# An involution and two Winograd convolutions on one core: involution by halves, low parts on VectorE, batch-norm sums on ScalarE

## The chip, the core and the metric

The kernel runs on 1 core of one Trainium2 chip. The time is that of one execution on the device, in microseconds. The core's engines are TensorE (PE, with PEld for its weight loads), VectorE (DVE), ScalarE (ACT), GpSimd (POOL) and SyncE (SP, which here only issues DMAs). Each engine runs its own list of instructions in order and waits on semaphores for the others.

## What is computed

Input x has 8 images of 256 channels, 56 x 56, in float32. Two residual blocks follow each other, each on a group norm of its input.

```python
def gn(v):                                  # 32 groups of 8 channels
    g = v.reshape(B, 32, C // 32, H, W)
    return ((g - mean(g)) / sqrt(var(g) + 1e-5)).reshape(v.shape)

def involution(x):                          # K = 7, G = 16 groups of 16 channels
    ker = einsum('bchw,oc->bohw', x, w_reduce) + b_reduce        # 64 channels
    ker = einsum('bchw,oc->bohw', ker, w_span) + b_span          # 16 * 49 channels
    ker = ker.reshape(B, 16, 1, 49, H, W)
    patches = all 49 shifts of pad(x, 3), reshaped to (B, 16, 16, 49, H, W)
    return (ker * patches).sum(axis=3).reshape(B, C, H, W)

def tri_conv(x, w):                         # 3 x 3, padding 1
    tq = ternary_quantize(w - mean(w))      # -1, 0 or 1, thresholds from max and min
    return conv(x, tq) + einsum('bchw,oc->bohw', x, tq[:, :, 1, 1])

def conv_block(x):
    out1 = relu(batch_norm(tri_conv(x, w1), g1, b1))             # over the whole batch
    return relu(out1 + batch_norm(tri_conv(out1, w2), g2, b2))

x = x + involution(gn(x))
x = x + conv_block(gn(x))
```

## The kernel before

The program goes through five stages. Everything is unrolled. Data dependencies become semaphores, and a scheduler puts each engine's instructions in order, near to the order of the text.

**Start.** `prep` of image 0, and `quantize` (L154) twice: it loads a weight tensor, finds the thresholds with DVE and POOL, makes the ternary weights, transforms them (six matrices a weight tensor, Winograd style) and stores them to DRAM (`wqd`). The working tile of `quantize` lies in the memory that the involution's `apool` and `qpool` take over afterwards.

**Involution (L578 to L609)**, by chunks: image b, channel tile t of 128 channels. The image is cut into patches of 3 x 8 pixels, 19 rows (`ty`) of 7 patches. A patch together with its border is 9 x 14 = 126 input pixels (`NQ`), which lie on the partitions. For each chunk:
- `generate` (L517) makes `a`, a [126, 133 patches, 8 groups x 24 pixels] tile: for every group and pixel of a patch the matrix that maps the 126 input pixels to the output pixel. It takes 32 steps. A step writes the products for three pixels and two groups (six float32 matmuls, L534, weights of 64 x 126, 133 columns each, two row halves of the array side by side; each float32 matmul is two load-and-multiply records in the trace) into one accumulator tile `pg`. DVE adds the bias on the way to `a` (L546), in every fourth step ACT does (L542).
- `apply_rows` (L552) then goes through ten pairs of patch rows. For each row it takes a tile `q` of 126 pixels x 7 patches x 128 channels, and 28 small matmuls (L560, weights 126 x 32, 48 columns). ACT (L568), DVE (L570) and POOL (L575) put the result onto x in SBUF.
- `load_q` (L508) loads a `q` tile, 441 KB in pieces of 512 bytes, from `xed`, a copy of the normed image in DRAM in which neighbouring patches' borders are repeated. It is issued on SP; six tiles are in hand (`NQB`).
- `prep` (L451), for the next image, runs in ten strips of six rows, one after each apply step of the chunk t = 1: POOL norms the strip (L457), PE reduces it to `kr` (L463, ACT L476), transposes it (L481, ACT L486), ACT's queue stores it to `xtd` (L489), and `expand` (L441), on SP, copies it into `xed`, DRAM to DRAM, two strips later.
- `params` (L405) computes the next image's group norm in two apply steps of the chunk t = 0; `group_norm_params` (L120) at the chunk's end computes that of the result (seven `bn_stats` on DVE, L124, two tiny matmuls, L128 and L135, and some DVE operations), and the result goes to DRAM (`x1d`, L609).

All accumulators of the stage come from one pool of four tiles (L388).

**Convolutions 1 and 2 (`conv_phase`, L214).** 16 half images each. `transform` (L243) norms the half image into `xp` with ACT (L619 or L629), builds six combinations of rows `r` with DVE (L261, L281 to L295), and `keep` (L263) splits each into a rounded high part `hi` (ACT, L266) and the rest `lo` (POOL, L267). The transform of half n + 1 is spread over the matmuls of half n. For each of the six, 24 matmuls (L343, 128 x 128, 392 columns) fill one of four accumulators; ACT copies two of them out (`e`, L350), DVE combines them to the output `y` (L353 to L369), takes its statistics (L375, eight `bn_stats`), and SP stores it (L377). The batch norm follows from the statistics (`batch_norm_params`, L142), once all halves are done.

**Final pass (L637 to L649).** It reads y1, y2 and x1, and writes the output.

## Time and profile before

| | us |
|---|---|
| median of 3 runs (2721.05 to 2726.63) | 2722.48 |
| the profiled execution | 2720.13 |
| its span, first to last instruction | 2718.0 |
| PE busy | 1841.0 |
| DVE busy | 1835.3 |
| ACT busy | 913.3 |
| POOL busy | 734.2 |

The profile's page gives for each engine its busy time, and a list of the costliest groups of instructions: source line, engine, operation, output tile and inputs, shapes, number, then busy time and the mean duration of one in ns, and after the bar the time that the engine stood idle just before them, with what ended it. A tile's name stands without its buffer number, so `pa` are all accumulators of apply. "issue" as a releaser means that the engine waited for nothing that the profile shows. In a timeline a row has its start and its length in us, the engine, line, tiles and the number of instructions merged into it, and in brackets the idle time before it. PEclk is the granted clock of TensorE as a share of full speed; the DMA share is the mean busy share of the core's 16 DMA engines.

### The profile page before, as it was taken

The numbers are of one execution on the slowest core, as the hardware profiler recorded it, in microseconds if no ns is written. First come the engines' busy times: TensorE is split into PE (matmuls) and PEld (weight loads), VectorE is DVE, ScalarE is ACT, GpSimd is POOL, SyncE is SP. The second block draws the span as 40 slices with busy tenths as digits, with TensorE's granted clock in tenths as the row PEclk, the third lists the DMA queues.
The fourth block names the chain that finished last, engine by engine and source line by source line (L and its number), as shares of the span: only waits on it lengthen the run. The fifth ranks groups of instructions, "written<-read, shape, count | busy, mean of one in ns | idle before, by whom it ended". The sixth has DMA issues, their size and how long they took to land.

```text
span 2718.0 us, 65147 instructions
## 1 busy us (share of the span) xinstructions
PE 1841.0 (68%) x28676; PEld 1727.9 (64%) x28676; DVE 1835.3 (68%) x2499; ACT 913.3 (34%) x1819; POOL 734.2 (27%) x701
## 2 busy tenths in 40 slices
PE   3147667687776768777648899998499898992000
PEld 2137566676665667666548889898498898992000
DVE  4575354564644455553449999999599999995444
ACT  2023324243342434333223433333143333422333
POOL 2001212121121212112115444454154454440000
PEclk9567879788786878778779999999799999996555
DMA  6436786767678576757763233221423222217998
GB/s 238 177 123 168 227 229 191 225 193 232 174 236 241 173 230 190 232 151 226 198 189 115 97 117 123 98 97 72 166 93 119 103 97 97 98 79 313 428 429 382
DMA packets 343531, 500.64 MB, mean 184 GB/s; under 512 B 11496, under 2 KB 308678, under 8 KB 327314
## 3 DMA queue, kind: packets, MB, share of 16 engines
q1 hardware_dynamic: 306320, 424.76, 47.4%
q10 hardware_dynamic: 36930, 71.74, 7.0%
q8 instruction: 225, 3.69, 0.6%
q14 instruction: 56, 0.46, 0.1%
HBM read 353.49 MB, written 187.92 MB: 199 GB/s over the span
## 4 chain that ended last, share of the span: by engine, by line
PE 31%; DVE 31%; DMA 17%; issue 15%; ACT 3%; POOL 1%; SPq 1%; ACTq 0%; DVEq 0%; POOLq 0%
PE pg L534 14%; PE pa L560 9%; DMA q<-xed 5%; DVE y L329 4%; DVE st L375 4%; DVE a L261 3%; PE c L343 3%; PE pk L463 3%; DMA y1f<-y1d 3%; DVE r L295 3%; DVE r L261 2%; DMA out_y<-x1f 2%; DMA x1f<-x1d 2%; PE pt L481 1%; DVE y L360 1%
## 5 line engine op out<-in xcount | busy, mean ns | idle before, releaser
L343 PE MATMUL c<-pl,wq 128*128 128x392 f32 x4608 | 909.7, 362 | 142.6 <-ACT e L350 79.3
L343 PEld LDWEIGHTS c<-pl,wq 128*128 128x128 f32 x4608 | 896.1, 199 | 155.9 <-ACT e L350 89.1
L267 POOL TENSOR_TENSOR pl<-r,pl 128x812 fp32r<-128x812 f32 x192 | 469.2, 2468 | 525.5 <-ACT pl L266 448.9
L560 PE MATMUL pa<-a,q 126*32 126x48 f32 x17024 | 316.1, 244 | 275.2 <-issue 200.4
L560 PEld LDWEIGHTS pa<-a,q 126*32 126x32 f32 x17024 | 280.2, 138 | 311.8 <-issue 251.6
L534 PE MATMUL pg<-kr,wl 64*126 64x133 f32 x6144 | 403.6, 293 | 40.3 <-DVE a L546 35.5
L534 PEld LDWEIGHTS pg<-kr,wl 64*126 64x126 f32 x6144 | 394.6, 200 | 46.4 <-DVE a L546 35.8
L570 DVE SCALAR_TENSOR_TENSOR inv<-pa,half_sb,inv 128x168 f32<-128x168 f32 x304 | 105.7, 388 | 446.5 <-ACT inv L568 446.3
L546 DVE TENSOR_TENSOR a<-pg,bt 126x798 f32<-126x798 f32 x384 | 370.5, 1044 | 25.9 <-PE pg L534 13.1
L575 POOL TENSOR_TENSOR x<-x,inv 128x168 f32<-128x168 f32 (+1 forms) x304 | 156.2, 533 | 765.5 <-DVE inv L570 761.2
L266 ACT CAST pl<-r 128x812 fp32r<-128x812 f32 x192 | 166.7, 871 | 494.6 <-DVE r L281 342.1
L542 ACT ACTIVATE a<-pg,bt 126x133 f32<-126x133 f32 x768 | 230.3, 482 | 288.5 <-PE pg L534 187.2
L568 ACT ACTIVATE inv<-pa,half_sb 128x336 f32<-128x336 f32 (+1 forms) x160 | 84.2, 526 | 474.6 <-PE pa L560 469.9
L457 POOL TENSOR_SCALAR xn<-x,gn 128x336 f32<-128x336 f32 (+1 forms) x160 | 95.9, 608 | 314.9 <-PE pt L481 251.1
L261 DVE SCALAR_TENSOR_TENSOR a<-xp 128x812 f32<-128x812 f32 x64 | 173.2, 2738 | 0.0
L463 PE MATMUL pk<-xn,wr 128*128 128x336 f32 (+1 forms) x320 | 131.2, 540 | 25.9 <-POOL xn L457 23.2
L375 DVE BATCH_NORM_STATS2 st<-y 128x6 f32<-128x392 f32 x256 | 122.6, 549 | 0.0
L124 DVE BATCH_NORM_STATS2 st_b<-x 128x6 f32<-128x448 f32 x112 | 69.7, 623 | 73.5 <-POOL x L575 73.4
L629 ACT ACTIVATE xp<-raw,bi_bn,sc_bn 128x392 f32<-128x392 f32 (+1 forms) x128 | 84.7, 720 | 65.8 <-DVE a L261 51.1
L619 ACT ACTIVATE xp<-raw,gn 128x392 f32<-128x392 f32 (+1 forms) x128 | 84.5, 720 | 53.8 <-DVE a L261 45.2
L476 ACT ACTIVATE kr<-pk,br 128x112 f32<-128x112 f32 (+1 forms) x232 | 74.6, 455 | 80.1 <-PE pk L463 79.3
L646 DVE SCALAR_TENSOR_TENSOR y1f<-y2f,sc_bn,y1f 128x3136 f32<-128x3136 f32 x16 | 55.7, 3484 | 65.5 <-DMA y2f<-y2d 65.5
(115 smaller groups left out, 1508.5 us busy)
## 6 DMA issues: line engine op xcount, KB each, us to landing
q<-xed SPq DMA_DIRECT2D x304, 441.0 KB
xed<-xtd SPq DMA_DIRECT2D x72, 588.0 KB
xtd<-stg ACTq DMA_DIRECT2D x72, 384.0 KB
raw<-x1d SPq DMA_DIRECT2D x32, 812.0 KB
raw<-y1d SPq DMA_DIRECT2D x32, 812.0 KB
x<-in_x SPq DMA_DIRECT2D x16, 1568.0 KB
x1d<-x SPq DMA_DIRECT2D x16, 1568.0 KB
y1d<-y SPq DMA_DIRECT2D x32, 784.0 KB
```

The lines of the kernel that those rows point to most:

```text
L261: nc.vector.scalar_tensor_tensor(dst, x, c, y, ALU.mult, ALU.add)
L266: nc.scalar.copy(hi, r)
L267: nc.gpsimd.tensor_tensor(lo, r, hi.bitcast(F32), ALU.subtract)
L329: nc.vector.scalar_tensor_tensor(yr[k][:, to], x[:, to], c, z[:, to], ALU.mult, op)
L343: nc.tensor.matmul(ps[:, to, :NM], wq[:, k, t, dx, to * P:(to + 1) * P], part[:, t, :, dx:dx + W], start=(c == 0), stop=(c == last))
L375: nc.vector.bn_stats(stats[:, to, n * NST + j, :], y[:, to, j * NM:(j + 1) * NM])
L463: nc.tensor.matmul(pk[:, :n * W], wr[:, t, :], strip[:, t, :n, PAD:PAD + W], start=(t == 0), stop=(t == CT - 1))
L534: nc.tensor.matmul(dst, wl[rows, t, gp, o:o + NQ], kr[rows, py, px].rearrange("r a t -> r (a t)"), start=True, stop=True)
L542: nc.scalar.activation(av[:, g0 + h, p0 + j], ps[:NQ, h, j * NT:(j + 1) * NT], AF.Identity, bias=bt[:, t, g0 + h, p0 + j:p0 + j + 1])
L546: nc.vector.tensor_tensor(av[:, g0:g0 + 2, p0:p0 + 3].rearrange("q g p t -> q g t p"), ps[:NQ, :, :3 * NT].rearrange("q h (t p) -> q h t p ...
L560: nc.tensor.matmul(ps[g * 32:(g + 1) * 32, r, k * 2 * NP:(k + 1) * 2 * NP], q[:NQ, k, g * 32:(g + 1) * 32], a[:NQ, (ty + r) * TX + k, g * ...
L575: nc.gpsimd.tensor_tensor(xv, xv, inv[:, r].rearrange("p t (y x) -> p y t x", y=PY)[:, :m], ALU.add)
```

## The change

Involution: `a` is made for one half of a chunk at a time (10 or 9 patch rows, 70 or 63 patches; two tiles, `a0` and `a1`, of together the same size). `generate` becomes a generator of 16 steps: six pixels and two groups a step, in 12 matmuls of 70 or 63 columns; DVE takes five of the six pixels (one instruction), ACT the sixth (two). The main loop runs over halves. After each apply step of a half it advances `generate` of the next half by three or four steps, then a side task: `params` of the next image, now for both channel tiles at once and cut into five pieces (chunk t = 0, second half), or the strips of `prep` (chunk t = 1: one a step in the first half, two, two, one in the second). `kr` is split into two tiles by halves. `expand` copies a half image in one DMA, so there are two per image, issued in the last half after apply steps 1 and 4. The result's `bn_stats` follow the apply steps; its aggregate and the store to `x1d` come after the first apply step of the next half; the group norm of the result is computed once, for all images, at the end. Five `q` tiles are in hand instead of six, and the first loads of the next image are put on SP at the end of the chunk before. The first half's `generate` stands between the two `quantize`.

Convolutions: `lo` is subtracted on DVE. The eight `bn_stats` of a half image are replaced by four ACT passes over `y` (sum and sum of squares of y less a shift, the shift being the mean of one block of the first half image), one after each of the first four groups of matmuls of the next half (ahead of the copy `e`, where there is one). `batch_norm_params` works from the sums.

The core of the diff (context lines shortened):

```diff
-NT = TY * TX
+HTY = (10, 9)
...
-NQB = 6
+STEPS = 5
+UP, UV = 6, 5
+NU = GP * NP // UP
+NQB = 5
...
+    def image_stats(st, xt, j):
+        nc.vector.bn_stats(st[:, j, :], xt[:, j * NC:(j + 1) * NC])
...
+    def batch_norm_params(stats, shift, gamma, beta, name):
         mv = small.tile([P, CT, 2], F32, tag="bn_mv", name=f"bmv_{name}")
-        for t in range(CT):
-            nc.vector.bn_aggr(mv[:, t, :], stats[:, t, :, :].rearrange("p n s -> p (n s)"))
+        nc.vector.tensor_reduce(mv, stats, AX.X, ALU.add)
+        nc.vector.tensor_scalar(mv, mv, 1.0 / (B * HW), None, ALU.mult)
+        d = small.tile([P, CT], F32, tag="bn_d", name=f"bd_{name}")
+        nc.vector.tensor_tensor(d, mv[:, :, 0], mv[:, :, 0], ALU.mult)
+        nc.vector.tensor_tensor(mv[:, :, 1], mv[:, :, 1], d, ALU.subtract)
+        nc.vector.tensor_tensor(mv[:, :, 0], mv[:, :, 0], shift, ALU.subtract)
...
                 nc.scalar.copy(hi, r)
-                nc.gpsimd.tensor_tensor(lo, r, hi.bitcast(F32), ALU.subtract)
+                nc.vector.tensor_tensor(lo, r, hi.bitcast(F32), ALU.subtract)
...
+        def statistics(n, y):
+            if n == 0:
+                mv = small.tile([P, CT, 2], F32, tag="sh_mv", name=f"sh_mv{i}")
+                for to in range(CT):
+                    st = small.tile([P, 6], F32, tag=f"sh_st{to}", name=f"sh_st{i}_{to}")
+                    nc.vector.bn_stats(st, y[:, to, :NM])
+                    nc.vector.bn_aggr(mv[:, to, :], st)
+                nc.vector.tensor_scalar(shift, mv[:, :, 0], -1.0, None, ALU.mult)
+            for to in range(CT):
+                for j, f in enumerate((AF.Identity, AF.Square)):
+                    dummy = wk.tile([P, NH], F32, tag="dummy", name=f"dummy{i}_{n}_{to}_{j}")
+                    nc.scalar.activation(dummy, y[:, to], f, bias=shift[:, to:to + 1],
+                                         accum_out=stats[:, to, j, n:n + 1])
+                    yield
+        done = iter(())
...
+                next(done, None)
                 if k in (2, 4):
                     e = half("e")
                     nc.scalar.copy(e, m[k])
...
-                for j in range(NST):
-                    nc.vector.bn_stats(stats[:, to, n * NST + j, :],
-                                       y[:, to, j * NM:(j + 1) * NM])
                 nc.sync.dma_start(dst_d[b][to][:, h * NH:(h + 1) * NH], y[:, to])
+            done = statistics(n, y)
+        for _ in done:
+            pass
...
+        def expand(b, h):
             src, dst = xt_d[b % 2][:], xe_d[b % 2][:]
-            n = min(SR, H - s * SR)
+            r0 = h * HTY[0] * PY
+            n = min(HTY[h] * PY, H - r0)
             nc.sync.dma_start(
-                bass.AP(dst.tensor, dst.offset + (PAD + s * SR) * QX * C,
-                        [[EX * C, TX], [QX * C, n], [1, QX * C]]),
-                bass.AP(src.tensor, src.offset + s * SR * WQ * C,
-                        [[PX * C, TX], [WQ * C, n], [1, QX * C]]))
-        def prep(b, pr):
+                bass.AP(dst.tensor, dst.offset + (PAD + r0) * QX * C,
+                        [[QX * C, n], [EX * C, TX], [1, QX * C]]),
+                bass.AP(src.tensor, src.offset + r0 * WQ * C,
+                        [[WQ * C, n], [PX * C, TX], [1, QX * C]]))
...
-                if s > 1:
-                    expand(b, s - 2)
                 yield
-            expand(b, NS - 2)
-            expand(b, NS - 1)
-        prm = [params(0, t, xs[0, t]) for t in range(CT)]
-        for _ in prep(0, prm):
-            pass
-        with tc.tile_pool(name="qp", bufs=1) as qp:
-            quantize(wq_d[0], w1, qp, ps_flat, "w1")
-            quantize(wq_d[1], w2, qp, ps_flat, "w2")
...
+        def generate(b, t, h, a):
+            n = HTY[h] * TX
             av = a[:NQ].rearrange("q t (g p) -> q g p t", g=GT)
+            for u in range(NU):
+                gp, p0 = u // (NP // UP), u % (NP // UP) * UP
+                ps = ps_tile(f"pg_{b}_{t}_{h}_{u}")
+                for j in range(UP):
                     py, px = (p0 + j) // PX, (p0 + j) % PX
                     o = LEAD - py * QX - px
+                    for i in range(2):
+                        rows = slice(i * CR, (i + 1) * CR)
+                        dst = ps[:NQ, i, j:UV * n:UV] if j < UV else ps[:NQ, i, j * n:(j + 1) * n]
                         nc.tensor.matmul(
                             dst, wl[rows, t, gp, o:o + NQ],
+                            kr[h][rows, py, px].rearrange("r a t -> r (a t)"),
                             start=True, stop=True)
                 g0 = 2 * gp
+                nc.vector.tensor_tensor(
+                    av[:, g0:g0 + 2, p0:p0 + UV].rearrange("q g p t -> q g t p"),
+                    ps[:NQ, :, :UV * n].rearrange("q i (t p) -> q i t p", p=UV),
+                    bt[:, t, g0:g0 + 2, p0:p0 + UV].unsqueeze(2).to_broadcast([NQ, 2, n, UV]),
+                    ALU.add)
+                for j in range(UV, UP):
+                    for i in range(2):
+                        nc.scalar.activation(
+                            av[:, g0 + i, p0 + j], ps[:NQ, i, j * n:(j + 1) * n],
+                            AF.Identity, bias=bt[:, t, g0 + i, p0 + j:p0 + j + 1])
+                yield
...
+        queue = [(b, t, ty) for b in range(B) for t in range(CT) for ty in range(TY)]
         loads = {}
         def prefetch(b):
-            while queue and queue[0][0] == b and len(loads) < NQB:
+            while queue and queue[0][0] <= b and len(loads) < NQB:
...
+        for _ in params(0):
+            pass
+        for _ in prep(0):
+            pass
+        for h in range(2):
+            expand(0, h)
+        apool = ph1.enter_context(tc.tile_pool(name="apool", bufs=1))
+        a_next = apool.tile([P, HTY[0] * TX, GT * NP], F32, tag="a0", name="a_0_0_0")
+        with tc.tile_pool(name="qp", bufs=1) as qp:
+            quantize(wq_d[0], w1, qp, ps_flat, "w1")
+            for _ in generate(0, 0, 0, a_next):
+                pass
+            quantize(wq_d[1], w2, qp, ps_flat, "w2")
+        apool1 = ph1.enter_context(tc.tile_pool(name="apool1", bufs=1))
+        qpool = ph1.enter_context(tc.tile_pool(name="qpool", bufs=NQB))
+        halves = [(b, t, h) for b in range(B) for t in range(CT) for h in range(2)]
+        pending = None
+        prefetch(0)
+        for m, (b, t, h) in enumerate(halves):
+            a = a_next
+            gen = iter(())
+            if m + 1 < len(halves):
+                b1_, t1_, h1_ = halves[m + 1]
+                a_next = (apool, apool1)[h1_].tile([P, HTY[h1_] * TX, GT * NP], F32,
+                                                   tag=f"a{h1_}", name=f"a_{b1_}_{t1_}_{h1_}")
+                gen = generate(b1_, t1_, h1_, a_next)
+            if h == 0:
+                st = small.tile([P, NCB, 6], F32, tag="gn_st2", name=f"st2_{b}_{t}")
+                gst[b, t] = (st, 0)
             more = b + 1 < B
+            side, plan = iter(()), (0,) * STEPS
+            if more and t == 0 and h == 1:
+                side, plan = params(b + 1), (1, 1, 1, 1, 1)
+            elif more and t == 1 and h == 0:
+                strips = prep(b + 1)
+                side, plan = strips, (1, 1, 1, 1, 1)
+            elif more and t == 1:
+                side, plan = strips, (2, 2, 1, 1, 0)
+            for i in range(STEPS):
+                apply_rows(b, t, h, a, i)
                 prefetch(b)
+                statistics(b, t, h * HTY[0] + i * QG)
+                if i == 0 and pending is not None:
+                    pending()
+                    pending = None
+                if more and t == 0 and h == 0 and i == 0:
+                    for k in range(CT):
+                        xs[b + 1, k] = load_x(b + 1, k)
+                advance(gen, 4 if i == 0 else 3)
+                advance(side, plan[i])
+                if more and t == 1 and h == 1 and i in (1, STEPS - 1):
+                    expand(b + 1, int(i > 1))
+            for _ in gen:
                 pass
+            for _ in side if (t, h) != (1, 0) else ():
+                pass
+            if h == 1:
+                pending = finish(b, t)
+                prefetch(b + 1 if t == 1 else b)
+        pending()
+        for _ in group_norm_params(mv2.rearrange("p b t s -> p (b t) s"),
+                                   gn2.rearrange("p b t s -> p (b t) s"), ps_flat, "gn2"):
```

## The prediction

> **What bounds the kernel now.** I read the page first, then the sums by stretch of time, cut where the chain of waits changes its kind (first weight quantization to 172 us, involution to 1409, convolution 1 to 1952, convolution 2 to 2467, final pass).
>
> ```profile
> 0.00:172.00 172.00, 32.54 (x156) 24.85 (x156) 94.86 (x118) 18.66 (x43) 15.06 (x31) 0.67 0.51 191
> 172.00:1409.00 1237.00, 897.69 (x23908) 805.95 (x23908) 645.45 (x1258) 427.43 (x1230) 238.52 (x444) 0.80 0.70 201
> 1409.00:1952.00 543.00, 457.29 (x2308) 450.48 (x2308) 492.84 (x553) 186.69 (x258) 244.30 (x116) 0.91 0.30 117
> 1952.00:2467.00 515.00, 453.50 (x2304) 446.66 (x2304) 484.45 (x524) 185.91 (x256) 236.36 (x111) 0.93 0.27 100
> 2467.00:2718.00 251.00, 0.00 (x0) 0.00 (x0) 117.68 (x48) 94.60 (x33) 0.00 (x0) 0.50 0.98 414
> ```
>
> Columns: stretch, its length, busy PE, PEld, DVE, ACT, POOL, granted clock, DMA share. The convolutions are DVE's: 977 of 1058 us busy, with PE at 911. In the involution no engine is full: PE 898 of 1237, DMA 0.70. The final pass is DMA at 0.98, and the change leaves it alone. So the groups by shape for the convolutions, and the timeline of PE for the involution.
>
> ```profile
> L267 POOL TENSOR_TENSOR pl<-r,pl 128x812 fp32r<-128x812 f32 x192 | 469.2, 2468 | 525.5 <-ACT pl L266 448.9 <-DMA raw<-y1d 56.3 <-PE c L343 20.3
> L261 DVE SCALAR_TENSOR_TENSOR a<-xp 128x812 f32<-128x812 f32 x64 | 173.2, 2738 | 0.0
> L375 DVE BATCH_NORM_STATS2 st<-y 128x6 f32<-128x392 f32 x256 | 122.6, 549 | 0.0
> L295 DVE SCALAR_TENSOR_TENSOR r<-u,v 128x812 f32<-128x812 f32 x32 | 77.3, 2415 | 0.0
> L261 DVE SCALAR_TENSOR_TENSOR q<-xp 128x812 f32<-128x812 f32 x32 | 32.5, 1017 | 2.6 <-ACT xp L619 1.7 <-ACT xp L629 0.9
> ```
>
> One DVE form on one shape takes 1.02 us (q) where POOL is idle and 2.74 us (a) where POOL's L267 runs: the difference is waiting for POOL, not work.
>
> ```profile
> 591.56 1.29 PE L560 MATMUL pa<-a,q 126*32 126x48 f32 x98 [1.36 <-issue]
> 598.34 1.22 PE L560 MATMUL pa<-a,q 126*32 126x48 f32 x94 [3.11 <-issue]
> 604.87 1.16 PE L560 MATMUL pa<-a,q 126*32 126x48 f32 x89 [1.30 <-issue]
> 609.21 1.13 PE L560 MATMUL pa<-a,q 126*32 126x48 f32 x85 [0.72 <-issue]
> ```
> ```profile
> 536.49 2.79 PE L560 MATMUL pa<-a,q 126*32 126x48 f32 x127 [3.42 <-issue]
> ...
> 547.02 2.79 PE L560 MATMUL pa<-a,q 126*32 126x48 f32 x128 [1.09 <-issue]
> ```
> ```profile
> 1377.90 2.86 PE L560 MATMUL pa<-a,q 126*32 126x48 f32 x128 [2.51 <-issue]
> ...
> 1405.99 1.04 PE L560 MATMUL pa<-a,q 126*32 126x48 f32 x75 [2.09 <-issue]
> ```
>
> In the apply stretches PE runs 128 matmuls (each with its weight load, 256 instructions), then stands without a wait that the profile knows. The page's instruction queue q8 moved 225 packets in 3.69 MB, one per 255 PE instructions: PE waits for its own program. From one such start to the next it takes 5.9 us under the load of 591 to 609 (17.65 us in 3 steps), 5.3 us from 536.49 to 547.02 (two steps, the one between at 541.81), and 4.7 us in the last chunk (28.09 us in 6 steps), where DMA is lighter. PE idles 200 us on "issue" ahead of L560, and only 60 on the q tiles.
>
> **The change, part by part.**
>
> Convolutions. (a) The low parts leave POOL for DVE: 192 subtractions at 0.99 us (L281, the same operation and shape on DVE) add 190 us. Bounds: 0.91 us, DVE's spacing in a row, and 2.47 us, POOL's price; the operands are L281's, so 0.99. (b) With POOL silent, the inflated forms fall back to their quiet twins: L261 a 64 x (2.74 - 1.02) = 110, L295 32 x (2.42 - 1.10) = 42, L329 y from s 64 x (0.98 - 0.55) = 27, L360 32 x (1.18 - 0.97) = 7: 186 us. (c) The batch-norm statistics, 123 us, leave DVE. DVE falls by 186 + 123 - 190 = 119 us over 32 half images: from 30.5 to 26.8 us each. (d) ACT gains four passes over 1568 columns per half image. No row has that width or an accumulated sum; L629 takes 0.75 us for 448 columns and L645 3.00 for 3136, which puts 1568 at 1.69 (between 0.75 and 3.00); 4 x 1.69 = 6.8 on top of 11.6 (373 / 32) is 18.4 us, covered by PE's period. If it is not covered, copy e (L350) comes up to 1.7 us later, and PE waits for it. (e) PE's 144 matmuls take 28.34 us:
>
> ```profile
> 1654.00 28.34 PE L343 MATMUL c<-pl,wq 128*128 128x392 f32 x144 [2.39 <-ACT e L350]
> ```
>
> Its period now is 31.26 us ((1904.41 - 1498.07) / 13 between two such starts). PE becomes the bound; each subtraction now holds DVE until ACT's cast (0.87 us) is done, and behind it in DVE's order stand the sums s and d that free PE's accumulators; with DVE at 26.8 of 28.3 some waiting stays: 29.1 us, between 28.4 and 31. That is 31 x 2.16 = 67, plus 4 at the two first half images: **-71 us** (ends -90 and -5). The new end of the statistics, 4 x 1.69 us on ACT after the last y, lies under the 17.25 us store of y1 and the reload, as the 3.6 us of aggregation do now.
>
> Involution. (f) Generate works on 70 or 63 columns instead of 133, so there are twice as many matmuls: 768 records per (b, t) where there were 384, each with a load of the same 126 weight columns. What does such a record cost? Ends: 64 ns (24.74 us / 384, nothing saved) and 32 ns (half the columns, half the time). The nearest row is the reduction: L463 starts 285 ns apart at 336 columns, and 111 ns at 112, where 285 x 112 / 336 is 95: under some 130 columns the load sets the pace. Two row halves run at once, so 111 / 2 = 55 ns. PE's streaming per image: 2 x 768 x 0.055 = 84, apply 2 x 1064 x 0.0128 (L560's quick bursts, 2.07 us for 162) = 27, strips 10 x (1.41 + 0.82) = 22: 134 us at full clock (0.80 is granted there now, with the idle time; at 0.9 it is 149). (g) The program grows from 2 x (384 + 1064) + 96 = 2992 to 2 x (768 + 1064) + 96 = 3760 pairs per image, from 23.4 to 29.4 packets. Now 6 of the 23.4 are generate's, at 8.2 us each and thus never late. After it every packet holds some of the 12.8 ns pairs, and takes 134 / 29.4 = 4.55 us to run on average, less than most refills. So refills set the pace: 29.4 x 5.3 = 156 us, where 5.3 is the mean of 5.9, 5.3 and 4.7. Ends: 134 (never late) and 29.4 x 5.9 = 173. (h) What still waits: at an image's end the second expand DMA waits on the SP queue for the last strip, and the first q loads stand behind it; now that hole is 14.8 us (generate ends at 665.0, PE takes the first q at 679.8). The second expand can start two steps before the half ends: 7 us, between 0 and 15. The x1 store and, behind it, the next image's x loads move one step later on SP; the loads wait for the store (45 us in all now, 8 each) and hold up the q loads behind them, but the five q tiles in hand last two steps of 8 us: nothing; uncovered, 8 us an image. The GroupNorm chains on PE (78 us of waits for gnp now) are spread over steps, hence nothing. So 163 us per image against 157 now ((1237 - 136) / 7; the last image, without strips, took 136). The last image: 25.6 packets x 4.7 = 120; first q loads, uncovered, 8. Stage: 7 x 163 + 120 + 8 = 1269, **+32 us** (ends: 7 x 134 + 110 = 1048, -189, and 7 x 188 + 145 = 1461, +224).
>
> The Trainium skill, "Runtime: NRT & Kernel Launch", Instruction fetch mechanics, says that the sequencer fetches the next 16 KiB block while it runs the current one, and that the cost is mostly hidden. The rows above show the block's size (3.69 MB / 225), but 200 us of idle time that is not hidden. By the page the stage would be PE's streaming alone, 7 x 141 + 120 = 1107 us, 162 less than by the rows; I keep to the rows.
>
> (i) The other engines stay covered: DVE's evacuations grow from 24 x 0.955 = 23 to 16 x (0.85 + 0.78) = 26 us per (b, t) (700 and 630 columns at L546's rate), 87 us per image; ACT 57, POOL 30, DMA 0.70 x 157 = 110, all under 163. If PE were quicker, DMA at 110 would be the next bound. Five q buffers for six take one load (1.8 us of DMA) off the lead, nothing while refills rule.
>
> Start. (j) The first half's generate moves between the two quantizations: 16 x 0.85 = 13.6 us of DVE beside the 25 us in which DVE waits for the second weights (101 to 121 us); without that cover it costs 13.6. I take **+3**.
>
> Sum on the profiled execution's span: 2718 - 71 + 32 + 3 = 2682; 2.1 us lie around the span (2720.13), and the median of the runs is 2.3 above that execution: **2686**.
>
> **Rivals.**
> B, refills come quicker. The load on DMA is spread evenly (0.70 in place of 0.95 in half of the apply stretches), and 4.7 us of the last chunk becomes the rule: 29.4 x 4.7 + 7 = 145 per image, stage 1135, time 2718 - 71 - 102 + 3 + 4 = 2552. For: the wait depends on load. Against: of my three samples one.
> C, the other side: the instruction stream takes the place of the generate stretch that is removed. Its point is a mean refill of 5.5 us: stage 1237 + 68 eats the convolutions' gain (7 x (29.4 x 5.5 + 7) + 120 + 8 = 1309). At 5.9 us: 7 x 180.5 + 25.6 x 5.3 + 8 = 1407, time 2718 - 71 + 170 + 3 + 4 = 2824. For: the loaded sample, and 48 more packets. Against: the DMA load falls on average.
> D, the convolutions don't gain: ACT's four passes stand ahead of copy e, or DVE waits for each cast before its subtraction, and the period stays at 31: 2718 + 32 + 3 + 4 = 2757. For: PE already waits for e (79 us). Against: ACT is at 35%.
>
> **How the numbers follow.** A (my forecast, refills of 5.0 to 5.5 us) 0.55, its own range 2623 to 2726; B 0.14; C 0.18; D 0.13. Time 2686. What this kernel's measurement can tell from no change is 0.2%, 5.4 us; 0.07 of A's chance lies there. Faster: 0.48 + 0.14 = 0.62; same 0.07; slower 0.18 + 0.13 = 0.31. The range 2580 to 2800 leaves out about half of B and half of C.
>
> **What would show it.** Convolutions: L261 a at about 1.0 us, POOL near 0, runs of 144 matmuls starting 29 us apart; D if they still start 31 apart. Involution: some 48 more q8 packets; records of generate 55 ns apart; "issue" as PE's first cause of idle time in every step, at 29 packets per image. A generate record at 32 ns, or idle time that goes to q tiles or DVE instead, would prove (f) to (h) wrong.

## The result and the profile after

The changed kernel takes 2802.22 us (median of 4 runs, 2794.43 to 2810.32) against 2724.36 for the kernel before (4 runs, 2721.05 to 2726.63): 1.0287 times the time, 95% interval 1.0253 to 1.0322. It is slower, where the forecast was 2686 us and faster. The profiled execution took 2810.32 us, its span 2808.5.

The same five stretches of the changed kernel, in the columns of the prediction's first fence (stretch, length, busy PE, PEld, DVE, ACT, POOL, granted clock, DMA share and GB/s):

```profile
0.00:192.00 192.00, 68.80 (x592) 61.82 (x596) 106.84 (x121) 27.41 (x73) 15.09 (x31) 0.66 0.48 177
192.00:1643.00 1451.00, 1309.28 (x29537) 1223.06 (x29528) 640.90 (x1106) 472.74 (x1432) 238.74 (x444) 0.78 0.58 171
1643.00:2111.00 468.00, 429.09 (x2308) 428.34 (x2308) 417.05 (x529) 287.04 (x386) 10.04 (x20) 0.96 0.36 136
2111.00:2557.00 446.00, 429.60 (x2304) 428.21 (x2304) 411.92 (x501) 281.01 (x377) 2.94 (x15) 0.98 0.31 115
2557.00:2808.00 251.00, 0.00 (x0) 0.00 (x0) 112.78 (x46) 100.48 (x41) 0.00 (x0) 0.51 0.98 415
```

For exact sums I cut by PE's own events. Before, the first apply matmul starts at 194.5 us, the first convolution matmul at 1431.4, the last at 2464.0; after, at 189.8, 1664.9 and 2555.1 (with the hundredths kept in the differences that follow). So the way to the first apply is 4.6 us shorter, the involution from there to the first convolution 238.1 longer (1236.9 to 1475.0), the convolutions 142.4 shorter (1032.6 to 890.2), the final pass 0.6 shorter: +90.5 us, the difference of the two spans. The convolutions gained twice what was forecast, and the involution lost all of that and more.

The costliest groups of the page after (line, engine, operation, output and inputs, shapes, count; busy us and mean ns; idle time before them and its cause):

```profile
L563 PE MATMUL pg<-kr,wl 64*126 64x70 f32 (+1 forms) x12288 | 935.0, 319 | 39.9 <-issue 28.3
...
L375 PE MATMUL c<-pl,wq 128*128 128x392 f32 x4608 | 857.5, 348 | 51.4 <-ACT pl L281 32.8
...
L588 PE MATMUL pa<-a,q 126*32 126x48 f32 x17024 | 283.2, 231 | 161.2 <-DMA q<-xed 100.1
...
L338 ACT ACTIVATE dummy<-y,nc 128x1568 f32<-128x1568 f32 x128 | 205.3, 1604 | 15.6 <-DVE y L361 14.3
L282 DVE TENSOR_TENSOR pl<-r,pl 128x812 fp32r<-128x812 f32 x192 | 186.4, 997 | 29.9 <-ACT pl L281 29.0
```

Generate is the change: 404 us of PE before (L534 on the old page, 376 from the first apply on), 935 now (893 from the first apply on). PE in the involution is busy 1313 us in place of 877 (+436) and idle 162 in place of 360 (-198): the interleaving does take away idle time, as it was meant to. "issue", the wait for the instruction stream, fell from 203 to 88 us and is still the first cause; the small group norm matmuls no longer wait (59 us before); q waits fell from 60 to 48. The 100.1 us ahead of L588 on the page also hold 51.9 us in which PE stands before its very first apply matmul, in the start. The second row below is one of the seven image ends, which cost 4.3 to 9.2 us each:

```profile
189.84 2.56 PE L588 MATMUL pa<-a,q 126*32 126x48 f32 x112 [51.94 <-DMA q<-xed]
...
713.85 1.50 PE L588 MATMUL pa<-a,q 126*32 126x48 f32 x56 [6.64 <-DMA q<-xed]
```

But PE's own work grew by twice what the idle time shrank. Part of that is the doubled number of records; the rest shows in PE's timeline, with no wait in it:

```profile
738.68 7.94 PE L563 MATMUL pg<-kr,wl 64*126 64x63 f32 x72
746.55 2.47 PE L588 MATMUL pa<-a,q 126*32 126x48 f32 x112
748.95 7.94 PE L563 MATMUL pg<-kr,wl 64*126 64x63 f32 x72
756.82 2.47 PE L588 MATMUL pa<-a,q 126*32 126x48 f32 x112
```
```profile
846.54 0.82 PE L526 MATMUL pt<-ident_sb,xn 128*128 128x128 f32 x6
847.28 1.40 PE L588 MATMUL pa<-a,q 126*32 126x48 f32 x112
848.61 4.24 PE L563 MATMUL pg<-kr,wl 64*126 64x63 f32 x72
```

The same 72 records take 7.9 us in one place and 4.2 us in the other; from start to start inside such a run they stand 107 and 55 ns apart, the second as in step (f). The sums of two such stretches:

```profile
738.70:781.00 42.30, 42.30 (x661) 41.23 (x661) 18.30 (x32) 9.08 (x28) 4.13 (x8) 0.50 0.35 89
```
```profile
841.00:877.00 36.00, 35.59 (x867) 31.99 (x864) 16.64 (x28) 17.78 (x51) 11.08 (x20) 1.00 0.67 205
```

In the first, PE is busy for all of 42.30 us and is granted half its clock throughout. In the second, where strips of the next image (pk, pt) stand between, it has the full clock. By the granted clock in the trace, 649 of the involution's 1475 us are at half clock, and 3580 of its 11904 generate records begin in them: at 107 ns in place of 55, these alone cost 186 us (the other 384 records, the first half's, stand in the start). PE is busy for 572 of the 649 us. If all of that ran at twice the speed, PE's 1313 us would be 1026, an estimate.

### The profile page after: what moved, and what is told of

Its sections match the earlier page's. It is cut to its first block, busy times and chain, and to the rows that moved or that the text cites. A ratio compares the mean times of both kernels' runs of the same rounds, so it can differ in the third digit from the quotient of the medians.

```text
span 2808.5 us, 77451 instructions
## 1 busy us (share of the span) xinstructions
PE 2236.8 (80%) x34728; PEld 2141.4 (76%) x34728; DVE 1689.5 (60%) x2303; ACT 1168.7 (42%) x2308; POOL 266.8 (10%) x509
## 4 chain that ended last, share of the span: by engine, by line
PE 75%; DMA 16%; issue 4%; DVE 4%; ACT 0%; SPq 0%; POOL 0%; ACTq 0%; DVEq 0%; POOLq 0%
PE c L375 30%; PE pg L563 30%; PE pa L588 9%; PE pk L508 4%; DMA q<-xed 4%; DMA x1f<-x1d 3%; DMA y1f<-y1d 2%; DMA out_y<-x1f 2%; PE pt L526 2%; DVE x1f L738 1%; DMA y1d<-y 1%; DMA w_w<-in_w 1%; DMA y2f<-y2d 1%; DMA wq<-wqd 0%; DMA xed<-xn 0%
## 5 line engine op out<-in xcount | busy, mean ns | idle before, releaser
L563 PE MATMUL pg<-kr,wl 64*126 64x70 f32 (+1 forms) x12288 | 935.0, 319 | 39.9 <-issue 28.3
L563 PEld LDWEIGHTS pg<-kr,wl 64*126 64x126 f32 x12288 | 904.2, 233 | 57.4 <-issue 31.6
L375 PE MATMUL c<-pl,wq 128*128 128x392 f32 x4608 | 857.5, 348 | 51.4 <-ACT pl L281 32.8
L375 PEld LDWEIGHTS c<-pl,wq 128*128 128x128 f32 x4608 | 855.6, 189 | 53.1 <-ACT pl L281 33.5
L568 DVE TENSOR_TENSOR a<-pg,bt 126x630 f32<-126x630 f32 (+1 forms) x512 | 431.3, 847 | 358.2 <-PE pg L563 353.2
L575 ACT ACTIVATE a<-pg,bt 126x63 f32<-126x63 f32 (+1 forms) x1024 | 298.5, 373 | 770.6 <-DVE a L568 769.5
L588 PE MATMUL pa<-a,q 126*32 126x48 f32 x17024 | 283.2, 231 | 161.2 <-DMA q<-xed 100.1
L588 PEld LDWEIGHTS pa<-a,q 126*32 126x32 f32 x17024 | 250.1, 128 | 188.3 <-issue 169.3
L338 ACT ACTIVATE dummy<-y,nc 128x1568 f32<-128x1568 f32 x128 | 205.3, 1604 | 15.6 <-DVE y L361 14.3
L282 DVE TENSOR_TENSOR pl<-r,pl 128x812 fp32r<-128x812 f32 x192 | 186.4, 997 | 29.9 <-ACT pl L281 29.0
L128 DVE BATCH_NORM_STATS2 st<-x 128x6 f32<-128x448 f32 x224 | 133.1, 618 | 58.7 <-DMA x<-in_x 42.3
L508 PEld LDWEIGHTS pk<-xn,wr 128*128 128x128 f32 x320 | 62.6, 222 | 66.8 <-POOL xn L502 41.9
```

Source lines behind the costliest of these rows:

```text
L128: nc.vector.bn_stats(st[:, j, :], xt[:, j * NC:(j + 1) * NC])
L282: nc.vector.tensor_tensor(lo, r, hi.bitcast(F32), ALU.subtract)
L338: nc.scalar.activation(dummy, y[:, to], f, bias=shift[:, to:to + 1], accum_out=stats[:, to, j, n:n + 1])
L375: nc.tensor.matmul(ps[:, to, :NM], wq[:, k, t, dx, to * P:(to + 1) * P], part[:, t, :, dx:dx + W], start=(c == 0), stop=(c == last))
L508: nc.tensor.matmul(pk[:, :n * W], wr[:, t, :], strip[:, t, :n, PAD:PAD + W], start=(t == 0), stop=(t == CT - 1))
L563: nc.tensor.matmul(dst, wl[rows, t, gp, o:o + NQ], kr[h][rows, py, px].rearrange("r a t -> r (a t)"), start=True, stop=True)
```

## What grants the clock: a count in the traces

The stretches of equal clock last multiples of 3.41 us (6.83, 10.24, 13.65 us ...), so the trace can be cut into windows of that length. For each window I added up how much of the array works: over the matmul records beginning in it, columns x 0.85 ns (285 ns for the strips' 336 columns) x rows / 128 x output columns / 128, as a share of 3.41 us. Generate alone gives 0.25 at half clock, because 63 columns occupy the array for half of the time that the next 126 weight columns take to load; at full clock it gives 0.51. With 133 columns, before the change, it gives 0.46 at half clock in the first such window (172.8 us) and 0.94 at full. Counted over the involutions of six kernels, the last four of them experiments below (windows at half clock and how many of them were followed by full clock; windows at full clock and how many were followed by half):

```
share of array      below 0.36          0.36 to 0.42        over 0.42
                 half  up full down    half  up full down   half  up full down
before             97   4   52   49      20  13   16    3     34  34  144    0
after             155   0   27   27      24  18   12    3     12  12  203    0
before_split      441   3   49   48      23  19    8    1     29  27   57    0
early_q           124   0   35   35      28  24   10    0     12  11  210    0
tail91             48   0   26   24      41  15   12    4     13  13  265    0
tail126            20   0   26   24       5   2    7    1     24  23  304    0
```

Below 0.36 the clock almost never rises (7 of 885) and nearly always falls; over 0.42 it nearly always rises (120 of 124) and never falls. That is theory 1: the clock follows the worked share of the array. The counts shift by a few with how a record at a window's edge is taken; in tail91 some twenty half-clock windows of nearly the same share lie within 0.01 of the 0.36 line and can stand on either side of it, and none of them rose.

The weighting matters. One border on this share, at 0.363, tells the next window's clock in all but 54 of the six kernels' 2607 windows. The best border on columns alone, without rows and output columns, misses 294, and the best on the share of time in which PE is busy misses 817 ("the same clock as now" misses 436). So it is neither PE's idle time nor its streaming time by itself that the clock follows.

Generate's short streams have two steady states: at full clock they work 0.51 of the array and keep it; after any wait that drops the clock they work 0.25 and can't get it back, however long PE is busy. In the changed kernel's involution the clock rose 30 times, each time after a window with strips or with at least 84 apply records in it, never after generate alone. The kernel before had the same gate, and its trace shows the same border, but its 133 columns lifted the clock by themselves (at 172.8 us for one).

The Trainium skill, "TensorE: Matmul & The Clock Gate", What's actually happening, has a window of 3413 ns and a gate that activity releases; the trace agrees on the window. Its working rule in HAM oscillation, no idle gaps over about 3.4 us, doesn't cover this case: 42.3 us without a gap ran at half clock.

The rivals: theory 2, refills of the instruction stream set the pace (the forecast's own reason); theory 3, only the number of records costs, and the clock follows idle time; theory 4, a form of it, the long holes at the images' ends hold the clock down.

## The experiments

Those with an interval against the kernel before are medians of four runs; the others (up3, before_split, tail91, stats_act, lo_dve) are one run each, beside runs of the kernel before with medians of 2720 to 2723 us.

**conv_only: the involution of before with the convolutions of after.** `conv_phase` and `batch_norm_params` are after's, all else is before's.

> The involution of before with the convolutions of the change (low parts on DVE, statistics on ACT). If the two parts of the change are independent, the convolutions take the 914 us they take after (1643 to 2557 us) in place of 1058, and the involution stays at 1237: 2720 - 144 = 2576 us. If part of the convolutions' gain comes from the involution's new order or from the batched GroupNorm, it lands between 2600 and 2720. By the forecast's own step (a period of 29.1 us) it would be 2650.

2582.2 us, 0.9481 of before (0.9465 to 0.9497). The convolutions take 890.2 us, as after; the involution 1242.3 as before. The two parts are independent, and this kernel is faster than both.

**up3 and up3_dup: the same records, with more work in each.** A step has three pixels in place of six, to make room in the accumulator. Here, and in tail126 and tail91 below, DVE takes three steps of four whole and ACT the fourth (these lines are left out). up3 has this alone; up3_dup also streams every column twice.

```diff
-UP, UV = 6, 5
+UP = 3
 # up3_dup only:
+src = src.unsqueeze(1).to_broadcast([CR, 2, n])
+dst = ps[:NQ, i, :2 * UP * n].rearrange("q (d t p) -> q d t p", d=2, p=UP)[:, :, :, j]
 nc.tensor.matmul(dst, wl[rows, t, gp, o:o + NQ], src, start=True, stop=True)
...
-advance(gen, 4 if i == 0 else 3)
+advance(gen, 8 if i == 0 else 6)
```

> The changed kernel with generate in units of 3 positions in place of 6 (32 units of 12 row-half matmuls' halves each, three of four evacuated by DVE, one by ACT); same matmuls, same streams of 70 or 63 columns. It is the control for up3_dup. Every theory: 2780 to 2840 us, involution's granted clock 0.78 as after; DVE and ACT are not the bound. If the evacuation had been the pace, it would differ by more than 30 us.

> up3 with each generate matmul streaming its 70 or 63 columns twice (the second copy lands in unused columns of the same accumulator and is never read): same records, same loads, more work for TensorE. Theory 1 (the clock gate looks at how much of the array works in a window of 3.4 us; generate's short streams at half clock are too little to get full clock back): the records at half clock now work 0.48 of the array in place of 0.25, so the clock comes back inside generate; granted clock of the involution at 0.88 or more, records 58 to 62 ns in place of 76 on average, the involution 1280 to 1340 us in place of 1451, the whole 2640 to 2710 us. Theory 2 (refills of the instruction stream set the pace): no change, 2800 us. Theory 3 (clock falls with idle time alone, and the doubled records cost their time): 12288 records become 6 to 10 ns longer, 2870 to 2930 us.

up3: 2793.0 us, involution 1442.5 at clock 0.80. up3_dup: 2663.95 us, 0.9788 of before (0.9771 to 0.9805), involution 1331.2 at clock 0.95. Twice the columns made the kernel 129 us faster than up3, its control. Theories 2 and 3 fall: the one expected nothing, the other a loss. Within theory 1's range the involution lies near the top, since 140 columns take longer than the load of 126 (72 records in 4.58 us, 64 ns each).

**before_split: the short streams alone, in the old order.**

```diff
+for c0, c1 in ((0, 70), (70, NT)):
     for h in range(2):
...
-        nc.tensor.matmul(dst, wl[rows, t, gp, o:o + NQ],
-                         kr[rows, py, px].rearrange("r a t -> r (a t)"), start=True, stop=True)
+        nc.tensor.matmul(dst[:, c0:c1], wl[rows, t, gp, o:o + NQ],
+                         kr[rows, py, px].rearrange("r a t -> r (a t)")[:, c0:c1], start=True, stop=True)
```

> The kernel before with nothing changed but generate's matmuls: each is issued as two, of 70 and 63 columns, in the old order (no interleaving, whole images, old convolutions). 6144 matmuls more. Theory 3 (only the record's price, 55 ns): 16 chunks of 768 x 55 = 42 us in place of 24.7: 2720 + 280 = 3000 us, all stretches at full clock once they run. Theory 1: a generate that begins at half clock stays there for its whole length, 768 x 109 = 84 us; with half or more of the 16 chunks beginning so, 3300 to 3650 us, at a granted clock of the involution under 0.70. Theory 2 (refills) has generate's own packets at 128 pairs x 55 ns = 7 us, never late: 3000 us.

3601.3 us. PE's timeline and the sums of that stretch:

```profile
968.09 81.27 PE L535 MATMUL pg<-kr,wl 64*126 64x70 f32 x768
```
```profile
968.00:1049.30 81.30, 81.30 (x773) 81.17 (x772) 26.28 (x33) 12.77 (x43) 0.00 (x0) 0.51 0.31 102
```

A whole chunk's generate, 768 records in one run without a wait, at half clock for 81 us: 106 ns each. The other chunks go the same way: 12244 of the kernel's 12288 generate records begin at half clock. Nothing but the cut of the streams differs from the kernel before, whose 384 records took 24.7 us. An unbroken run of short streams doesn't win the clock back, and no hole at an image's end is needed for that.

**tail126 and tail91: a dose.** Each matmul streams on into the columns that follow in the same buffer; the surplus results lie in columns that are never read. A step has four pixels. The two kernels differ in the number of columns alone.

```diff
-UP, UV = 6, 5
+UP = 4
+krf = [fixed([P, PY * PX * n * TX + 63], f"kr{h}") for h, n in enumerate(HTY)]
...
+src = krf[h][rows, (p0 + j) * n:(p0 + j) * n + 126]        # tail91: 91
+dst = ps[:NQ, i, j:UP * 126:UP]
...
-advance(gen, 4 if i == 0 else 3)
+advance(gen, 6 if i == 0 else 5)
```

> The changed kernel with every generate matmul streaming 126 columns: its own 70 or 63 and, behind them, the next ones in the same buffer, whose results fall into columns that are never read (units of 4 positions, so that they fit). Same records and loads. Where up3_dup streamed 140 columns for a load of 126 (64 ns per record against 58 for 126 columns), here the extra columns hide under the load. Theory 1 (clock by worked share of the array): clock of the involution 0.92 or more as in up3_dup, 5760 records 6 ns shorter, 35 us less than up3_dup: 2610 to 2650 us. If up3_dup won by its spacing of records and not by the array's work, or by the repetition of data, the clock falls back towards 0.8 and the time to 2700 or more.

> tail126 with 91 columns streamed per generate matmul in place of 126: a middle dose. At half clock a window of generate alone works 91 / 126 of what it does at 126 columns, about 0.34 of the array, just under the share (0.35 to 0.40) from which the traces show the clock rising; only windows that also hold a burst of apply are above it. Theory 1: clock and time between those of the changed kernel (0.78, 2802 us) and of tail126 (0.94, 2650 us): 0.84 to 0.92 and 2670 to 2740 us. If what helped in tail126 were the units of 4 or the buffer's layout, it would be at 2650; if the array's share did not matter below a full stream, at 2800.

tail126: 2650.3 us, 0.9745 of before (0.9725 to 0.9765), at the upper end of what was expected. tail91: 2722.2 us, involution 1378.8 at clock 0.88, between the two as expected. In the table tail91 has 41 half-clock windows between 0.36 and 0.42, of which 15 rose: at half clock its generate alone sits right at the border and stays there. tail126's involution, as sums, and PE's two large groups in it (51.4 of the 65.4 us at q are again the wait before the first apply):

```profile
186.40:1500.80 1314.40, 1124.37 (x29633) 1031.36 (x29633) 617.83 (x1189) 530.78 (x1939) 242.94 (x446) 0.94 0.66 196
```
```profile
L570 PE MATMUL pg<-kr,wl 64*126 64x126 f32 x11904 | 758.4, 282 | 52.4 <-issue 43.0 <-DVE a L579 4.5 <-ACT a L575 2.7
L594 PE MATMUL pa<-a,q 126*32 126x48 f32 x17024 | 252.4, 215 | 167.8 <-DMA q<-xed 65.4 <-issue 59.7 <-DVE a L579 30.6
```

Against after (1475.1 us, PE 1313, clock 0.78) the involution is 161 us shorter, with the same records and more columns. It is still 77 us longer than before: even at a granted clock of 0.94, generate's 758 us of PE against 376 is more than the interleaving gives back.

**early_q: the hole at an image's end.** After, the first q tiles of the next image are issued on SP behind the second expand. The changed kernel's chain of waits holds these loads at 14 to 15 us per image:

```profile
700.98 14.78 DMA q<-xed
...
900.14 14.54 DMA q<-xed
```

The expectation takes that for PE's wait. But PE still runs generate while such a load is under way: it waits 6.64 us at 713.85 (the row in the result section), 4.3 to 9.2 us at each of the seven ends, 45 us in all. The expectation's 100 us also hold the 51.9 us of the start.

```diff
-prefetch(b)
+prefetch(b + 1 if more and t == 1 and h == 1 and i > 1 else b)
```

> The changed kernel with one thing moved: in the last half of an image the loads of the next image's first q tiles are issued as buffers come free, ahead of the second expand on the SP queue, in place of behind it. The hole at each image's end (14 to 15 us of waiting for q, 100 us in all) should shrink to 0 to 5 us. Theory 1: the clock still falls at the short waits for instructions and stays at half in the first chunk of an image: 65 to 130 us less than the changed kernel, 2670 to 2740 us, clock 0.78 to 0.83. Theory 4 (it is the long idle gaps at an image's end that hold the clock down): without them the clock is 0.88 or more and the time under 2650 us.

2761.1 us (2745.8 to 2782.2), 1.0159 of before (1.0106 to 1.0212): 41 us less than after, below the 65 to 130 expected. Waits for q in the involution fell from 48 to 1 us and the involution by 48 (1475 to 1427); its clock was 0.80 in place of 0.78. Theory 4 falls: with practically all of the idle time at q gone, the clock doesn't come back. Short waits for instructions (after, 2.47 us at 737.39, in front of the half-clock stretch above) are enough to drop it.

**tail126_early: both.**

> Both edits. With the clock at full, generate 12288 x 58 ns = 713 us, apply 213, strips 148, waits for instructions some 110: 1190 us from the first apply to the first convolution in place of 1475, 2540 to 2590 us in all; below 2582 it beats the old involution with the new convolutions. If refills then set the pace at 29.4 blocks of 5.3 us an image, 156 us an image, 2600 to 2620.

2639.8 us, 0.9704 of before (0.9683 to 0.9726): a miss, only 10 us under tail126. There was little to win: tail126 waits only 14 us for q in the involution, and 3 are left here. PE is busy for 1117 us where the expectation's three terms add up to 1074, and it waits 107 us for instructions and 36 for DVE's a. The new involution with both repairs doesn't reach the old one.

**stats_act and lo_dve: the two parts of the convolutions' change.** In the kernel before, each alone: the statistics on ACT, or `lo` on DVE (`nc.gpsimd.tensor_tensor(lo, ...)` becomes `nc.vector.tensor_tensor(lo, ...)`).

> The kernel before with the batch norm statistics on ACT alone; the low parts stay on GpSimd. DVE loses 123 us of 977 but keeps the forms inflated by GpSimd (2.7 us for a, 186 us in all): 26.7 us per half image, below TensorE's 28.3. If DVE's total is the bound, nearly all of the convolutions' gain comes from this part: 2590 to 2640 us. If the waits for e and s, d behind the inflated forms hold TensorE, less: 2650 to 2720 us.

> The kernel before with the low parts alone moved from GpSimd to DVE; the statistics stay on DVE. By steps (a) and (b) of the prediction DVE gives up 186 us of inflation and takes on 190 us of subtractions: 30.6 us per half image as before, so DVE stays the bound, 2710 to 2730 us. If GpSimd's presence costs more than the inflation that the groups show (late accumulators, a lowered clock), the time falls below 2680 us.

stats_act: 2658.0 us, convolutions 964.1 in place of 1032.6, so the second of its two cases. lo_dve: 2684.3 us, convolutions 993.7, where steps (a) and (b) had no gain; DVE fell by 31 us (965.7 to 934.9), so, with 186 us of subtractions taken on, GpSimd's presence had cost 217 us of inflation and not 186. PE's group in lo_dve:

```profile
L343 PE MATMUL c<-pl,wq 128*128 128x392 f32 x4608 | 886.6, 354 | 126.8 <-ACT pl L266 81.6 <-ACT e L350 25.5 <-DMA wq<-wqd 19.4
```

Alone they gain 62 and 36 us (both against a median of 2720), together 141 (conv_only). Each alone leaves PE waiting in the convolutions (108 and 127 us); together 51 are left, all at the beginnings of the two stages, and inside the stages no wait remains that could drop the clock. DVE's total doesn't decide this by itself: in stats_act it is 849 us, already under PE's 875, and PE still waits, for e and for y among others; with both parts it is 818 under 857.

**conv_early and conv_gn_early: is there more to take from the change?** conv_only with the early q loads, and with the second group norm for all images at once.

```diff
-prefetch(b)
+prefetch(b + 1 if more and t == 1 and i > 6 else b)
 # conv_gn_early also:
-group_norm_params(xs[b, t], ps_flat, gn2[:, b, t, :], f"b{b}{t}")
+pending = finish(b, t)
```

> conv_only with the first q loads of the next image issued ahead of the last expands of the strips (as early_q does for the change). conv_only waits 51 us for q in the involution; if these waits are the SP queue's order, 30 to 50 us go: 2530 to 2555 us. If the q data are late for want of DMA bandwidth, nothing: 2582 us.

> conv_early with one more part of the change: the second GroupNorm for all images at once after the involution, its sums taken as rows become ready, in place of two small matmuls and a chain on DVE after each chunk. TensorE waits 50 us for those (38 and 12 us ahead of the two matmuls of gnp_b): 2480 to 2510 us. If the waits only hide other lateness (DVE's evacuations, POOL's sums), 2530 to 2555.

conv_early: 2571.2 us, 0.9444 of before (0.9416 to 0.9472), which overlaps conv_only's interval, so a gain over conv_only is not shown; q waits are 61 us against 51, not fewer. conv_gn_early: 2558.2 us, 0.9411 (0.9389 to 0.9432), the lowest median of the study, 244 us under the changed kernel's. Its involution is 1209.5 us, 22 less than conv_early's; the waits of gnp_b, some 45 us, are gone, but in the involution PE now waits 35 us for DVE's a, where conv_early has no such wait. Both expectations promised too much.

## Why the prediction was wrong

- **(f), generate's price, is the step that failed.** "55 ns each" was right at full clock (55 measured), and the records did double. What failed is the sentence "134 us at full clock (0.80 is granted there now, with the idle time; at 0.9 it is 149)". It took the clock for something that idle time lowers and that would rise as the idle time went. The clock follows the array's work, and the change halved the work of each record. Measured: PE busy 164 us per image (1313 / 8) at clock 0.78. A's own range, and rivals B to D, had no case in which the clock falls while PE is busy.
- **Size of the involution's loss.** The forecast's 1269 us are 1048 of PE's work (7 x 134 + 110) and 221 of waits; measured are 1475, with 1313 of work and 162 of waits. So PE's work is 265 us over the forecast and the waits are 59 under it: the whole miss is PE's work. With the half-clock time halved, PE's 1313 become 1026 (the estimate above), close to the 1048. tail126, at clock 0.94, has 1124.
- **(g), refills set the pace: refuted in the changed kernel.** The 49 more blocks came (274 for 225). "Issue" is PE's first cause of idle time, as forecast (88 us; q has 48), but at half of the forecast's size: 22 us per image and 10 in the last are 164. In tail126, at clock 0.94, it is 103. And PE's 164 us of work per image lie above the 156 us at which refills were to set the pace. The period of 5.3 us that I had read off was of a PE that ran through 128 pairs in 2.8 us or less and then waited. Mixed with generate, and at a lower clock, a block lasts 6.3 us on average (1475 / 234 blocks in that stretch). The rule cited there, from the Trainium skill, "Runtime: NRT & Kernel Launch", Instruction fetch mechanics, that the cost is mostly hidden, fits these 88 us better than it fitted the 203 us of the kernel before.
- **(h), the hole: right in size.** PE waits 4.3 to 9.2 us at an image's end, 6.4 on average, for 7 forecast. The reason given is not what happens: the second expand is still issued at the half's last step, not two steps earlier, and the q loads stand behind it on SP; moving them took 47 us off the waits. The group norm chains cost nothing, as said.
- **The rivals.** C's time, 2824 us, is close to the 2802 measured, but by chance: it holds longer waits for instructions, and these became shorter. B's stage sum leaves out the 8 us of the first q loads that A's has (1144, not 1135), which changes nothing here.
- **(j), the start.** The second quantization ended 13 us later (172.5 for 159.2 us on DVE), not 3; half-clock generate ran beside it. It cost nothing, because the first apply came 4.6 us earlier: the first half's matrices were ready, and PE stood 51.9 us for the first q tiles.
- **(a) to (d), right.** L276 a takes 0.995 us, `lo` 0.997, ACT's passes 1.60 plus 0.19 us for a separate record that reads the sum (1.69 forecast), all covered; POOL is silent. DVE fell by 147 us in place of 119, since more forms had been inflated than I added up. The Trainium skill, "SBUF — State Buffer", SBUF: two separate sides, has DVE operations with two SBUF inputs and GpSimd lock each other out for the whole instruction; the same form at 2.74 us beside GpSimd and 0.995 without agrees.
- **(e), right in kind, half in size.** PE became the bound, but at 26.7 us per half image, not 29.1. I took PE's 28.34 us for its floor:

```profile
1654.00 28.34 PE L343 MATMUL c<-pl,wq 128*128 128x392 f32 x144 [2.39 <-ACT e L350]
1685.72 4.62 PE L343 MATMUL c<-pl,wq 128*128 128x392 f32 x13 [3.38 <-ACT e L350]
```
```profile
1664.86 427.91 PE L375 MATMUL c<-pl,wq 128*128 128x392 f32 x2304 [18.37 <-DMA wq<-wqd]
```

Before (first fence), the first 13 matmuls after a wait take 355 ns each, half clock (the row ends with the view's window at 1690 us). After (second fence), 2304 matmuls run in one piece at 185.7 ns, 26.7 us per 144. The 28.34 held a window at half clock (1654.16 to 1657.58 us in the trace), which costs 1.6 us and came with the wait on e. Removing a wait of 2.4 to 3.4 us removed 4 to 5. Of the 2.4 us per half image by which 29.1 is too long, 1.6 are this window and 0.8 the waiting that the forecast left in place. Rival D, no gain, was far off.

So both sizes, all of the loss and two thirds of what the gain was short by, went wrong over one thing, the granted clock, which I had read from the rows as an average and carried over as a number.

## What to carry to other kernels

Before cutting a matmul's moving side in two, work out what share of the array the new shape keeps busy at half clock (columns streamed against weight columns loaded, times rows and output columns in use), and compare it with the share at which the clock rises in your own trace; a float32 stream shorter than its weight load can trap PE at half clock though it never waits. Where the cut can't be avoided, columns streamed for nothing up to the length of the load cost next to nothing at full clock and can win the clock back (152 us here with 126 columns; 129 with 126 and 140, the second of which is longer than the load). A busy time read behind a wait holds the slow start that the wait caused: take the floor of an engine from an unbroken run.

## What the hardware showed that was not expected

- In these kernels the granted clock follows the worked share of the array (columns x rows x output columns) in windows of 3.41 us, with a border between 0.36 and 0.42 of the full-clock capacity; of the table's 1183 full-clock windows over 0.42 none was followed by half clock.
- Streaming 126 columns in place of 63 or 70 behind a float32 load of 126 weight columns costs hardly anything at full clock: 80 records in 4.67 us (58 ns) in tail126, 72 in 4.17 (58 ns) after.
- In the changed kernel's involution each of the 11 waits of 1.5 to 3 us that began at full clock was followed by half clock (1.58 us at 796.75 and 2.47 us at 737.39 are two); of the 14 waits of 1 to 1.5 us, 5 were.
